# The layer norm's mean matmuls and factors moved behind the third backward tile in a two-way scan

## The chip, the cores and the metric

The kernel runs on one core of a Trainium2 chip. Its engines are TensorE (PE, with weight loads shown apart as PEld), VectorE (DVE), ScalarE (ACT), GpSimd (POOL) and SyncE (SP, which here only issues transfers); each works through its own instructions in order and waits for the others by semaphores. The metric is the device time of one execution in microseconds, as the median of three runs. Lower is better.

## The reference, cut to what matters

The program computes four residual blocks on x of shape (32, 192, 56, 56) in float32: an agent attention, an RWKV scan, a sparse shift with a 3x3 filter, and a long convolution. Each has a group norm ahead of it. The edit lies in the second block, the scan. With the tokens of an image in rows, N = 56*56 = 3136 of them and 192 channels:

```python
k, v, r = xs @ Wk.T, xs @ Wv.T, xs @ Wr.T          # xs: group-normed x
x_fwd = wkv_scan(real_w, u, k, v)                  # along the tokens
x_bwd = flip(wkv_scan(real_w, u, flip(k), flip(v)))
h = sigmoid(r) * 0.5 * (x_fwd + x_bwd)
mu, var = mean(h, -1), var(h, -1)                  # over the 192 channels
h = (h - mu) * rsqrt(var + 1e-5) * ln_g + ln_b
x = x + h @ Wo.T
```

The scan is a linear recurrence along the tokens: each output is a ratio of two running sums with decay exp(w), one of exp(k)*v and one of exp(k).

## The kernel before, in words

The stage is `scan_pairs` (from L898). Channels lie on the 128 partitions and tokens along the free axis. Images are taken in 16 pairs. One pair's 2 x 192 channels make three tiles of 128 partitions: tile 0 and tile 1 are the first 128 channels of the two images, tile 2 holds the last 64 channels of both. Tokens are cut into four chunks of 784 (MC), a chunk into two halves of 392 for PSUM's banks. A matrix product over channels comes in two parts: `outer` (L875) makes tiles 0 and 1, with lines L881 and L884, and `inner` (L886) makes tile 2, with L891 and L894.

Three generators or functions do the work of one chunk:

- `forwards` (L1135) loads x and normalises it on ACT (L1100), multiplies by Wk and Wv, takes exp(k) on ACT (L1149, tile `ek`) and exp(k)*v on DVE (L1154, tile `bv`), scans both (L1118, L1120 on DVE, with one-column copies on POOL at L1113 and L1119), inverts the denominator by a logarithm and an exponential on ACT (L1125, L1126) and multiplies (L1164).
- `backwards` (L1166) does the same from the right with the stored `ek` and `bv`, and takes the gate r: product with Wr, then three ACT operations (L1178, L1182, L1183) for the sigmoid. DVE then forms h in three operations per tile (L1186, L1187, L1188). It yields twice: after tiles 0 and 1, and after tile 2, "the third backward tile".
- `finish` (L1191) does the layer norm and the output product for the chunk that went through `backwards` a step earlier. It loads x, multiplies h by a centring matrix, squares on ACT (L1203, tile `sq`), multiplies the squares by a matrix of 1/192 (`mean_w`), makes the factors 1/sqrt(var) on ACT by a logarithm and an exponential (L1212, L1213, tile `rd`), and copies two 64-partition parts for tile 2 by transfers issued from ACT's queue (L1216). After a yield it multiplies h by the output matrix (`wog`), scales by the factors (L1226, DVE), adds bias and x with a running sum (L1229, DVE) and stores from SP's queue (L1243). It hands back functions that square the result on ACT (L1236) for the next block's group norm.

The main loop (from L1266) runs 16 pairs times four chunks, 64 steps; each step combines `backwards` of a chunk, `finish` of the chunk before and `forwards` of the next pair's chunk, in this order:

```python
next(back)
if ending is not None:
    next(ending)
next(back)
left = next(ending) if ending is not None else []
if ahead is not None:
    forwards(ahead, i, left)
```

In two of the four steps of a pair the group statistics of the pair before are gathered as well (L1079 to L1081, L1045 to L1048, L1026 to L1040), and once `conclude` stores them (L1250 to L1257).

This order is the one in which the operations are written. A scheduler orders each engine's instructions from it, by its own estimates, so neighbouring parts of one step are mixed on each engine. Tiles come from rotating pools: x from 7 buffers, `g`, `sq` and `rd` together from 9, PSUM from four buffers of two banks (`turned`). A load of x waits in SP's queue until the last reader of its buffer is done, and what stands behind it in that queue waits too.

Of the kernel before, what the change touches and what calls it, by code (L numbers as in the profile page):

```python
# [897 lines left out]
def scan_pairs(ctx: ExitStack, tc: tile.TileContext, a, k, x1, st_a, st_c, x2, rs2, wogT, count):  # L898
# [18 lines left out]
    def turned():  # L917
        ps = pp.tile([128, 2, BANK], F32, name="ps", tag="ps")
        return ps, ps[:, :, :HM], [ps[:, h, :HM] for h in range(2)]

    def parts(t):
        return [t[:, h * HM : (h + 1) * HM] for h in range(2)]
# [67 lines left out]
    def of(t):  # L990
        return slice(0, 1) if t < 2 else slice(1, 2)
# [13 lines left out]
    def load(p, m):  # L1005
        xs = [wp.tile([128, MC], F32, name="x", tag="x", bufs=7) for _ in range(3)]
        for r, t, ap in views(p, m):
            nc.sync.dma_start(out=xs[t][r], in_=ap)
        return xs
# [181 lines left out]
    def finish(s, m):  # L1191

        h, xs = s.y[m], load(s.p, m)
        hs = [parts(t) for t in h]
        sq = [wp.tile([128, MC], F32, name="sq", tag="t") for _ in range(3)]
        for tiles in ((0, 1), (2,)):
            ps = [turned() for _ in tiles]
            if len(tiles) == 2:
                pairs.outer(centre, [q[2] for q in ps], hs)
            else:  # L1200
                pairs.inner(centre, ps[0][2], hs)
            for t, (_, both, _) in zip(tiles, ps):
                nc.scalar.activation(  # L1203
                    sq[t].rearrange("p (h n) -> p h n", h=2), both, AF.Square,
                    accum_out=s.seen[:, 4, 3 * m + t : 3 * m + t + 1],
                )
        sqs = [parts(t) for t in sq]
        pv = [turned() for _ in range(2)]
        pairs.outer(mean_w, [q[2] for q in pv], sqs)
        rds = [wp.tile([128, MC], F32, name="rd", tag="t") for _ in range(3)]  # L1210
        for t, (_, both, _) in enumerate(pv):
            nc.scalar.activation(rds[t].rearrange("p (h n) -> p h n", h=2), both, AF.Ln, bias=eps)  # L1212
            nc.scalar.activation(rds[t], rds[t], AF.Exp, scale=-0.5)  # L1213

        for t, r in enumerate((slice(0, 64), slice(64, 128))):
            nc.scalar.dma_start(out=rds[2][r], in_=rds[t][r])  # L1216
        yield
        left = []
        for tiles in ((0, 1), (2,)):
            po = [turned() for _ in tiles]  # L1220
            if len(tiles) == 2:
                pairs.outer(wog, [q[2] for q in po], hs)
            else:
                pairs.inner(wog, po[0][2], hs)
            for t, (_, out, _) in zip(tiles, po):
                nc.vector.tensor_tensor(  # L1226
                    sq[t].rearrange("p (h n) -> p h n", h=2), out, rds[t].rearrange("p (h n) -> p h n", h=2), ALU.mult
                )
                nc.vector.scalar_tensor_tensor(  # L1229
                    xs[t], sq[t], cb[:, of(t)], xs[t], ALU.add, ALU.add, accum_out=s.sums[:, t, m : m + 1]  # L1230
                )
                if m == NM - 1:
                    nc.vector.tensor_scalar(s.away[:, t], s.sums[:, t, m : m + 1], -1.0 / MC, None, ALU.mult)

                def square(t=t):
                    nc.scalar.activation(  # L1236
                        sq[t], xs[t], AF.Square, bias=s.away[:, t], accum_out=s.squares[:, t, m : m + 1]
                    )

                left.append(square)  # L1240
        rows = slice(m * MC // S, (m + 1) * MC // S)
        for r, t, i, c in places:
            nc.sync.dma_start(out=x2[c, i, rows, s.p], in_=xs[t][r].rearrange("p (h w) -> p h w", w=S))  # L1243
        yield left
# [21 lines left out]
    for p in range(NP):  # L1266
        ahead = State(p + 1) if p + 1 < NP else None
        for i in range(NM):
            m = NM - 1 - i
            back, ending = backwards(s, m), None  # L1270
            if i > 0:
                ending = finish(s, m + 1)
            elif before is not None:
                ending = finish(before, 0)
# [7 lines that stand above are left out]
            else:  # L1282
                for later in left:
                    later()
            if before is not None:
                if i == 1:
                    before.spread = deviations(*moments_of(before), sp, "2")
                elif i == 2:
                    conclude(before)
        before, s = s, ahead  # L1290
    ending = finish(before, 0)
    next(ending)
    for later in next(ending):
# [587 lines left out]
```

## Time and profile before

| what | value |
|---|---|
| median of three runs | 12442.48 us (12437.2 to 12442.61) |
| the profiled execution's own time | 12448.77 us |
| its span, first to last instruction | 12447.0 us |
| granted TensorE clock, mean over the span | 0.96 |
| scan stage, start and end in the span | about 5052 to 8510 us |
| its regular part, 56 of the 64 steps | 5362 to 8350 us |
| transfers in that part | 99 GB/s, 0.40 of the DMA engines' time |

Times in the profile are microseconds from the span's start. An engine's row in the timeline gives start, length, engine, line, operation and the tiles it writes and reads; a bracket gives the idle time of the engine just ahead of the row and what ended it. Names stand without buffer numbers, so `ps` is any PSUM tile. Neighbouring instructions of an engine overlap by about 0.1 us, which is why a step from start to start is a little shorter than a length. The 56 steps form 14 rounds of four, and every round has the same order of instructions on DVE.

### The profile page before, as it was taken

How to read it: one execution, taken by the hardware profiler on the slowest of the kernel's cores; microseconds unless marked ns; L12 is line 12 of the kernel's file. 1: busy time of each engine (PE TensorE's matmuls, PEld its weight loads, DVE VectorE, ACT ScalarE, POOL GpSimd, SP SyncE). 2: the span in 40 equal slices, each digit the busy share in tenths (PEclk: the TensorE clock that was granted, in tenths of full speed). 3: DMA queues.
4: the chain of work that ended last, by engine and by line, in shares of the span. 5: the costliest groups of instructions: out<-in, count | busy, mean ns of one | idle time of the engine just before them, and what ended most of it. 6: DMA issues, size and time to landing. Idle time of an engine off the chain costs nothing. (4 is left out here: it accounts for less than half of the span.)

```text
span 12447.0 us, 164748 instructions
## 1 busy us (share of the span) xinstructions
PE 11356.6 (91%) x62738; PEld 7114.0 (57%) x62738; DVE 10861.2 (87%) x15560; ACT 6217.0 (50%) x11820; POOL 2303.7 (19%) x2237
## 2 busy tenths in 40 slices
PE   4999999999999999788888888888999999999999
PEld 1555555555555655333333333335777777777777
DVE  3888888888888888799999999997888888888888
ACT  2555555555555555466666666663333333333333
POOL 0000000000000000465555565552000000000000
PEclk7999999999999999899999999998999999999999
DMA  2111111111111111233444343432111111111111
GB/s 65 32 50 40 40 40 40 40 40 42 54 43 40 40 40 32 73 98 96 102 102 100 95 98 97 102 98 77 42 44 42 42 44 42 45 42 43 42 43 29
DMA packets 940870, 719.51 MB, mean 58 GB/s; under 512 B 777295, under 2 KB 818746, under 8 KB 931057
## 3 DMA queue, kind: packets, MB, share of 16 engines
q1 hardware_dynamic: 929832, 683.18, 21.3%
q10 hardware_dynamic: 10240, 25.70, 0.8%
q8 instruction: 500, 8.19, 0.3%
q14 instruction: 298, 2.43, 0.1%
HBM read 403.11 MB, written 240.80 MB: 52 GB/s over the span
## 5 line engine op out<-in xcount | busy, mean ns | idle before, releaser
L591 DVE SCALAR_TENSOR_TENSOR o<-v_a,dww,o 128x896 f32<-128x896 f32 (+1 forms) x1024 | 1056.9, 1032 | 408.1 <-ACT v_a L565 291.8
L1807 ACT COPY y<-ps 64x252 f32<-64x252 f32 (+1 forms) x2376 | 809.6, 341 | 1134.3 <-PE ps L1801 1104.0
L1725 PE MATMUL ps<-f,real 84*84 84x112 f32 x6144 | 1090.8, 259 | 0.0
L1725 PE MATMUL ps<-f,imag 84*84 84x112 f32 x6144 | 1089.4, 259 | 0.0
L1732 ACT COPY z<-ps 84x448 f32<-84x448 f32 x768 | 406.2, 529 | 1217.1 <-PE ps L1725 1215.6
L859 POOL MEMSET Wk_cc<- 128x128 f32 x1 | 0.2, 205 | 4819.7 <-DVE x_c L757 4819.7
L1725 PEld LDWEIGHTS ps<-f,real 84*84 84x84 f32 x6144 | 783.9, 153 | 134.2 <-issue 95.8
L1725 PEld LDWEIGHTS ps<-f,imag 84*84 84x84 f32 x6144 | 763.8, 153 | 0.0
L1125 ACT ACTIVATE q<-q 128x784 f32<-128x784 f32 x384 | 328.7, 856 | 808.9 <-DVE q L1120 637.8
L881 PE MATMUL ps<-sq,mean_aa 128*128 128x392 f32 x512 | 301.7, 753 | 424.6 <-ACT sq L1203 424.6
L591 DVE SCALAR_TENSOR_TENSOR o<-v_c,dww,o 128x448 f32<-128x448 f32 (+1 forms) x1024 | 638.5, 623 | 5.2
L604 PE MATMUL ps<-xs_a,gk_a 128*98 128x448 f32 (+1 forms) x1536 | 639.6, 497 | 0.0
L605 PE MATMUL ps<-xs_c,gk_c 125*98 125x448 f32 (+1 forms) x1536 | 633.1, 493 | 0.0
L608 ACT ACTIVATE pr<-ps,low 98x896 f32<-98x896 f32 (+1 forms) x384 | 352.3, 918 | 557.1 <-DVE low L606 557.1
L1591 POOL TENSOR_TENSOR mat<-tap,tap 114x114 f32<-114x114 f32 x96 | 40.8, 425 | 3166.6 <-PE ps L1651 2313.1
L696 PE MATMUL ps<-gq_a,xs_a 128*112 128x294 f32 x1792 | 603.3, 418 | 19.0 <-DVE pq L701 19.0
L1742 PE MATMUL ps<-z,f 84*114 84x448 f32 x1536 | 608.9, 539 | 0.0
L697 PE MATMUL ps<-gq_c,xs_c 125*112 125x294 f32 x1792 | 595.1, 413 | 0.0
L1699 PE MATMUL re<-y,f 128*84 128x420 f32 (+1 forms) x1152 | 532.2, 542 | 8.8 <-ACT y L1807 7.7
L1801 PEld LDWEIGHTS ps<-f,padded 114*128 114x128 f32 x3168 | 473.3, 192 | 96.7 <-issue 70.3
L1699 PE MATMUL im<-y,f 128*84 128x420 f32 (+1 forms) x1152 | 526.9, 538 | 0.0
L1801 PE MATMUL ps<-f,padded 114*128 114x168 f32 x3168 | 503.7, 310 | 21.6 <-DVE o L1744 10.2
(397 smaller groups left out, 29260.2 us busy)
## 6 DMA issues: line engine op xcount, KB each, us to landing
x<-x SPq DMA_DIRECT2D x512, 392.0 KB
x<-x SPq DMA_DIRECT2D x512, 196.0 KB
x<-x SPq DMA_DIRECT2D x192, 399.0 KB
out_x<-x SPq DMA_DIRECT2D x384, 196.0 KB
x_a<-in_x SPq DMA_DIRECT2D x32, 1568.0 KB
x<-x_a SPq DMA_DIRECT2D x32, 1568.0 KB
x_c<-in_x SPq DMA_DIRECT2D x64, 392.0 KB
x<-x_c SPq DMA_DIRECT2D x64, 392.0 KB
```

The lines of the kernel that those rows point to most:

```text
L591: nc.vector.scalar_tensor_tensor(dst, tap(i), dww[:, t, i : i + 1], dst, ALU.mult, ALU.add)
L604: mm(ps[P2, h, :n], g[:, cols], xs_a[j][:, px], start=True, stop=False)
L605: mm(ps[P2, h, :n], gk_c[0:KC, 2 * j + h, cols], xs_c[j][0:KC, px], start=False, stop=True)
L608: nc.scalar.activation(pr[:, :, :n], ps[P2, :, :n], AF.Exp, bias=low[:, j, p : p + 1], accum_out=sums[:, j, p : p + 1])
L696: mm(ps[:SUB, i, :HA], xs_a[j][:, px], g, start=True, stop=False)
L697: mm(ps[:SUB, i, :HA], xs_c[j][0:KC, px], gq_c[0:KC, 2 * j + (q + i) // ns], start=False, stop=True)
L1699: nc.tensor.matmul(ps[:, : n * 84], f2[:, i, :], y[:, i0 : i0 + n].rearrange("p g s u -> p (g s u)"), start=True, stop=True)
L1725: nc.tensor.matmul(ps[:84, i * 2 * S : (i + 1) * 2 * S], part[:, i0 + i].rearrange("p s u -> p (s u)"), f3[:, m, :], start=(m == 0), stop= ...
L1732: nc.scalar.copy(z[:, i0 : i0 + n].rearrange("p g m w -> p (g m w)"), ps[:84, : n * 2 * S])
L1742: nc.tensor.matmul(got, f4[:, m, :], z[:, i0 : i0 + n, m, :], start=(m == 0), stop=(m == 1))
L1801: nc.tensor.matmul(ps[:, g * 168 : (g + 1) * 168], flat[:, (g0 + g) * 128 : (g0 + g + 1) * 128], f1, start=True, stop=True)
L1807: nc.scalar.copy(y[64 * m : 64 * m + 64, 2 * g0 + i : 2 * (g0 + n) : 2], got[64 * i : 64 * i + 64, :, :, m, :])
```

## The change

One `yield` in `finish` moves up: from behind the factors and their copies to ahead of the mean's matmuls. So the first part of `finish`, written ahead of the third backward tile, now ends with the centring and the squares, and the mean's matmuls, the two logarithms and two exponentials and the two copies are written after that tile, just ahead of the output product.

```diff
                     sq[t].rearrange("p (h n) -> p h n", h=2), both, AF.Square,
                     accum_out=s.seen[:, 4, 3 * m + t : 3 * m + t + 1],
                 )
+        yield
         sqs = [parts(t) for t in sq]
         pv = [turned() for _ in range(2)]
         pairs.outer(mean_w, [q[2] for q in pv], sqs)
...
         for t, r in enumerate((slice(0, 64), slice(64, 128))):
             nc.scalar.dma_start(out=rds[2][r], in_=rds[t][r])
-        yield
         left = []
         for tiles in ((0, 1), (2,)):
```

In the changed kernel the lines of the moved part are one higher (L1213, L1214, L1217); from the output product on the numbers are as before. The scheduler works on the new order, so the order of neighbouring instructions on ACT, DVE and POOL changes as well.

## The prediction

> **What bounds the kernel now.** First the page, for the engines' shares; then the busy time by stage, to find the stage that the edit touches; then VectorE's (DVE's) waits inside it; last the timeline of one step, engine by engine.
>
> The page, first lines (busy us, share, instructions):
>
> ```profile
> span 12447.0 us, 164748 instructions
> ## 1 busy us (share of the span) xinstructions
> PE 11356.6 (91%) x62738; PEld 7114.0 (57%) x62738; DVE 10861.2 (87%) x15560; ACT 6217.0 (50%) x11820; POOL 2303.7 (19%) x2237
> ```
>
> PE leads over the whole, but the edit lies in the scan stage only. Busy time of its regular middle (start:end, length, then busy us by engine):
>
> ```profile
> 5362.00:8350.00 2988.00, 2485.15 (x9132) 1135.18 (x9130) 2903.91 (x2998) 1908.15 (x3278) 1725.80 (x1496) 0.93 0.40 99
> ```
>
> Here DVE is busy 2903.91 of 2988 us: the stage lasts as long as DVE's work, which the edit leaves alone, plus DVE's idle time, some 84 us. So the edit is worth what it does to DVE's waits there. These are (total, times, longest):
>
> ```profile
> DVE sq L1226 <- PE ps L884: 51.5, 39, 2.1
> DVE p L1186 <- ACT q L1126: 12.7, 22, 1.0
> DVE q L1118 <- ACT ek L1149: 10.2, 16, 0.7
> ```
>
> The stretch holds 14 rounds of four steps (A, B, C, D by how the third backward tile, tile 2, and the group statistics fall); rounds last 213.4 us on average (2988/14). A, B and D each wait once, 1.4 to 1.9 us, for the output product (wog, L884) or just after it; C hardly waits; B waits 0.7 more at L1118. One D step shows why. Its DVE, ACT and PE rows (start, length):
>
> ```profile
> 6822.72 0.94 DVE L1188 TENSOR_TENSOR y<-y,g 128x784 f32<-128x784 f32 x1
> 6823.59 1.02 DVE L1120 SCALAR_TENSOR_TENSOR q<-ek,eu,q 128x784 f32<-128x784 f32 x1
> 6826.30 0.97 DVE L1226 TENSOR_TENSOR sq<-ps,rd 128x784 f32<-128x784 f32 x1 [1.68 <-ACT g L1182]
> 6827.19 0.97 DVE L1186 TENSOR_TENSOR p<-p,q 128x784 f32<-128x784 f32 x1
> ...
> 6833.64 1.03 DVE L1229 SCALAR_TENSOR_TENSOR x<-sq,cb,x 128x784 f32<-128x784 f32 x1
> 6834.60 0.08 DVE L1229 DVE_READ_ACCUMULATOR x<-sq,cb,x 128x1 f32 x1
> 6834.63 3.60 DVE L1118 TENSOR_TENSOR_SCAN q<-decay,f,ek 128x784 f32<-128x784 f32 x2
> ```
> ```profile
> 6811.88 5.47 PE L881 MATMUL ps<-sq,mean_aa 128*128 128x392 f32 x8 [6.63 <-ACT sq L1203]
> 6817.28 1.59 PE L884 MATMUL ps<-sq,mean_ca 64*128 64x392 f32 x8
> 6818.80 1.58 PE L891 MATMUL ps<-x,Wr_cc 128*128 128x392 f32 x4
> 6820.31 1.54 PE L894 MATMUL ps<-x,Wr_ac 128*64 128x392 f32 x8
> 6821.78 2.90 PE L881 MATMUL ps<-y,wog_aa 128*128 128x392 f32 x8
> 6824.61 1.59 PE L884 MATMUL ps<-y,wog_ca 64*128 64x392 f32 x8
> ```
> ```profile
> 6824.65 0.86 ACT L1125 ACTIVATE q<-q 128x784 f32<-128x784 f32 x1 [1.08 <-DVE q L1120]
> 6825.41 0.84 ACT L1182 ACTIVATE g<-g 128x784 f32<-128x784 f32 x1
> 6826.16 0.84 ACT L1126 ACTIVATE q<-q 128x784 f32<-128x784 f32 x1
> ...
> 6832.75 0.95 ACT L1236 ACTIVATE sq<-x,away 128x784 f32<-128x784 f32 x1 [1.18 <-DVE x L1229]
> ```
>
> PE idles 6.63 us for the squares (L1203), then runs mean, Wr of tile 2 and wog in a row; wog ends at 6826.20, and DVE's L1226 starts at 6826.30 (the releaser named, L1182, ended just as late; the other steps name PE). But tile 2's reciprocal is hardly earlier: L1125, L1126, then DVE's L1186.
>
> **The change part by part.** No instruction is added or dropped; the built programs give the orders, here of a D step, with the tile in brackets (L1213, L1214, L1217 of the changed kernel are L1212, L1213, L1216 of the rows):
>
> ```
> DVE now  L1188(1) L1120(2) L1226(0) L1186(2) L1229(0) L1187(2) L1226(1) L1188(2) L1229(1) L1226(2) L1229(2) L1118
> DVE new  L1120(2) L1188(1) L1186(2) L1226(0) L1187(2) L1229(0) L1188(2) L1226(1) L1226(2) L1229(1) L1229(2) L1118
> ACT now  L1125(1) L1126(1) L1212 x2 L1213 x2 copies L1178(2) L1125(2) L1182(2) L1126(2) L1183(2) L1100 x2 L1236(0) L1100 L1236(1) L1149 x2 L1236(2)
> ACT new  L1125(1) L1178(2) L1126(1) L1182(2) L1100 L1183(2) L1213 x2 L1214(0) L1125(2) L1214(1) L1126(2) copies L1100 x2 L1236(0,1,2) L1149 x2
> ```
>  Steps are start to start, from the rows: DVE L1186, L1187, L1188, L1226 0.89 each, L1120 and L1229 0.95, scan 1.76; ACT 0.75 each, L1203 and L1178 0.80, L1100 0.94, L1236 0.95. Three latencies: L1125 starts 0.04 after L1120's end; L1186 0.97 after L1126 starts (6612.67 to 6613.64, where L1186 waited); L1118 0.93 after L1149 starts (6728.51 to 6729.44).
>
> *PE.* Tile 2's Wr goes ahead of the mean, into the 6.63 us gap. 1.58 + 1.54 us leave the stretch from squares to wog; L1226 would find wog 3 us sooner, so its wait on PE, up to 2.1 us, goes. Late next is ACT.
>
> A clock point, not needed below: the first eight mean matmuls take 5.47 us after the 6.63 us gap, the eight of wog 2.90. [...]
>
> *ACT, tile 2's reciprocal.* In A, B and D the new order is: L1178, L1126, L1182, L1100, L1183, (L1100), L1213 twice, then L1125 and L1126 of tile 2 with a factor's Exp (L1214) between; the factors stand ahead of it and end before DVE asks. From the end of tile 2's L1120, L1186 can start 0.04 + 0.76 + 0.75 + 0.97 = 2.52 later, as now, where L1182 stands between. DVE's new order puts L1186 ahead of L1226, and L1188 of tile 1 behind L1120 as sole cover, where L1226 used to stand. For D: L1120 at 6822.71 (L1188 of tile 1 now comes behind it), end 6823.73, L1188 ends its turn at 6824.52, L1186 starts at 6826.25: idle 1.73, against 1.68 now. A: 1.49 (L1257 covers 0.24), B 1.57 (L1048). C has L1253 and one L1226 as cover: 0.6, against 0 now. So **the wait on PE turns into a wait on ACT**.
>
> *ACT, the end of the step.* New on DVE: in A, B and D both last L1226 come ahead of both last L1229, so x of tiles 1 and 2 is finished late and close together. ACT squares them (L1236) ahead of the next state's exponential (L1149), in A and D all three squares first (now two). D on: L1186 6826.25, L1226 6827.14, L1187 6828.03, L1229 6828.91, L1188 6829.86, L1226 6830.75 and 6831.64, L1229 6832.53 and 6833.48. L1236 of tile 1 starts 1.07 after its L1229 (as 6831.68 to 6832.75): 6833.60; tile 2 6834.55; L1149 6835.50; L1118 6836.43. Now: 6834.63. **D loses 1.80 us**. The same working for the others:
> - A (L1120 at 6662.14): L1186 6665.69, last L1229 6672.91. Moments (L1080) now stand ahead of the scans and wait for the last L1236 (6673.98 to 6675.02): the five small operations end 0.87 later, both scans and L1120 take 5.37, L1154 at 6681.3 against 6680.55: +0.77.
> - B (6716.22): L1186 6719.77, last L1233 done 6728.15, L1236, L1149 6729.13, L1118 6730.06 against 6729.44: +0.62.
> - C: only the 0.6 at L1186: +0.60.
>
> A round: 3.79. These rows are of a round of 213.53, 0.12 over the mean, so 3.91; times 14, 54.7 us. The irregular steps: one before the 14 rounds is like D, +2; in the last backward step the 9.08 us wait of L1226 on PE shrinks by the 3 us of Wr: -3. **Sum +54 us.**
>
> *What stays hidden, with its bounds.* (1) L1100 of two forward tiles comes up ahead of the factors; its loads sit in SP's queue until tile 2's Wr has read the buffers (SP issues at 6714.25, Wr_cc ran 6712.59 to 6714.1). Wr moves up, so they are issued some 10 us sooner and land about 3.5 us later (issue 6775.09, L1100 in ACT 6778.56): cost 0. If they came no sooner than now, ACT would stand some 6 us past need, 1.5 of it slack: 4.5 x 56 = 250 us. I take 0, since the release moves. (2) The rd copies (ACT's queue, L1217) are issued after ACT passes tile 2's reciprocal, some 4.6 us ahead of the last L1226 in A and B; no row gives their landing apart. By the loads' 3.5 us they cost nothing; 1 us past need would cost 28 in A and B together. I take 0. (3) PSUM: wog of tile 1 takes Wr's bank, freed by L1178 before 6818: nothing.
>
> Against the runs: the profiled execution took 12448.77 (span 12447.0), 6.3 above the median 12442.48. So 12502.8 by its own time, 12496 on the scale of the runs.
>
> **Rivals.**
> 1. *Nothing takes the wait's place* (faster). DVE loses its waits at L1226, L1186 and L1118: 56.9 + 12.0 + 10.8 in the stretch, 3 at the end: 12360. It decides if L1186 of tile 2 can start within some 1 us of L1120's end. For: the PE wait is real and largest. Against: three ACT turns, 2.52 us, already show L1186 waiting 22 times.
> 2. *Only the exchange at L1186, the end of the step unharmed* (L1149 not behind the squares in time): A -0.27, B -1.16, C +0.60, D -0.01, so with the 0.12: -0.72 x 14 and -1: 12431, no change by measure. Against: ACT works in order, and A and D place three squares ahead.
> 3. *Loads late in ACT's queue*: +250 us, 12690. Against: (1) above.
> 4. *It does not do what it says*: the scheduler keeps the old order; 12442. Against: the built order has moved.
>
> **How the numbers follow.** Forecast 0.70, rivals 0.08, 0.15, 0.04, 0.03. Its own range is 12470 to 12530 (up: the copies late). The range leaves out rivals 1 and 3 (0.12) and reaches to rival 2: 12425 to 12530. 0.2%, 25 us, is about what a measurement can tell here: faster 0.09, same 0.17, slower 0.74.
>
> **What would show it.** Right: no wait of L1226 on PE; L1186 waits on L1126 in every A, B, D, about 1.5 us; L1118 waits on L1149 in B and D, L1080 on L1236 in A, 1 us; rounds of 217.3. Wrong: L1100 waiting on DMA, L1226 on the rd copy, or rounds of 208 to 213.

## The result, and the profile after

The changed kernel takes 12486.51 us (median of 6 runs, 12484.01 to 12499.9) against 12442.98 us (6 runs, 12437.2 to 12452.77): a ratio of 1.0037, 95% interval 1.0024 to 1.005, so it is slower by 30 to 62 us. It was run again later beside new runs of the kernel before (first experiment): 1.0039 (1.0025 to 1.0053).

The page of the changed kernel has nearly the engine times of before; DVE is 4.5 us less busy in a span 38 us longer:

```profile
span 12485.2 us, 164581 instructions
...
PE 11385.3 (91%) x62738; PEld 7095.6 (57%) x62738; DVE 10856.7 (87%) x15560; ACT 6203.9 (50%) x11820; POOL 2236.6 (18%) x2237
```

The same 56 regular steps, as one stretch (start:end, length, busy us of PE, PEld, DVE, ACT and POOL, then the granted clock, the DMA share and GB/s):

```profile
5352.00:8392.00 3040.00, 2525.22 (x9134) 1124.56 (x9134) 2900.35 (x2997) 1899.01 (x3277) 1664.45 (x1496) 0.96 0.40 97
```

DVE is busy about as long as before, 2900 us for 2904, and the stretch is 52 us longer: all of that is idle time of DVE, 140 us in place of 84. DVE's waits there (total, times, longest), first in the kernel before, over the 56 steps alone (the prediction's list began 62 us earlier, so two of its totals are a little larger), then in the changed kernel:

```profile
DVE sq L1226 <- PE ps L884: 50.8, 38, 2.1
DVE p L1186 <- ACT q L1126: 11.8, 21, 1.0
DVE q L1118 <- ACT ek L1149: 10.2, 16, 0.7
DVE sq L1226 <- ACT g L1182: 3.4, 2, 1.7
DVE sq L1226 <- ACT q L1125: 2.7, 3, 0.9
```
```profile
DVE p L1186 <- ACT q L1126: 72.3, 56, 1.6
DVE q L1118 <- ACT ek L1149: 51.8, 28, 1.9
DVE mv L1080 <- ACT sq L1236: 12.7, 14, 0.9
```

The wait of L1226 on PE is gone, and there are only waits on ACT. By place, L1226 and L1186 together waited 68.7 us before and L1186 waits 72.3 now, so that exchange is about even; the waits at the end of the step (L1118, L1080) grew from 10.2 to 64.5. A D step shows both places, DVE first (start, length, last bracket the wait):

```profile
6838.00 1.03 DVE L1120 SCALAR_TENSOR_TENSOR q<-ek,eu,q 128x784 f32<-128x784 f32 x1
6838.95 0.96 DVE L1188 TENSOR_TENSOR y<-y,g 128x784 f32<-128x784 f32 x1
6841.54 0.98 DVE L1186 TENSOR_TENSOR p<-p,q 128x784 f32<-128x784 f32 x1 [1.63 <-ACT q L1126]
6842.43 0.97 DVE L1226 TENSOR_TENSOR sq<-ps,rd 128x784 f32<-128x784 f32 x1
...
6848.76 1.03 DVE L1229 SCALAR_TENSOR_TENSOR x<-sq,cb,x 128x784 f32<-128x784 f32 x1
...
6851.70 3.59 DVE L1118 TENSOR_TENSOR_SCAN q<-decay,f,ek 128x784 f32<-128x784 f32 x2 [1.91 <-ACT ek L1149]
```

ACT and PE of the same step:

```profile
6839.06 0.86 ACT L1125 ACTIVATE q<-q 128x784 f32<-128x784 f32 x1 [1.65 <-DVE q L1120]
6839.83 0.84 ACT L1214 ACTIVATE rd<-rd 128x784 f32<-128x784 f32 x1
6840.57 0.84 ACT L1126 ACTIVATE q<-q 128x784 f32<-128x784 f32 x1
...
6849.83 0.95 ACT L1236 ACTIVATE sq<-x,away 128x784 f32<-128x784 f32 x1
...
6850.78 0.80 ACT L1149 ACTIVATE ek<-ps 128x784 f32<-128x784 f32 x1
```
```profile
6827.18 4.59 PE L881 MATMUL ps<-sq,mean_aa 128*128 128x392 f32 x8 [3.50 <-ACT sq L1203]
...
6836.05 1.59 PE L884 MATMUL ps<-y,wog_ca 64*128 64x392 f32 x8
```

PE has wog ready at 6837.64, almost 5 us before L1226 uses it at 6842.43; that gain shows in the rows. But DVE stands at L1186 for tile 2's reciprocal: three ACT operations behind L1120, with one DVE operation (L1188) to cover them. At the end of the step the last L1229 starts at 6848.76; ACT squares its result from 6849.83, turns to L1149 only at 6850.78, and DVE scans from 6851.70.

Steps start to start, means over the 14 rounds (regular part: 56 steps):

| | A | B | C | D | round | shortest and longest round | regular part |
|---|---|---|---|---|---|---|---|
| before | 54.06 | 54.18 | 51.99 | 53.18 | 213.41 | 212.90, 214.58 | 2987.7 |
| after | 54.82 | 55.01 | 52.40 | 54.90 | 217.13 | 217.11, 217.15 | 3039.8 |
| difference | 0.76 | 0.83 | 0.41 | 1.72 | 3.72 | | 52.1 |

The last but one column is a further sign that PE is off the path: before, rounds differed by up to 1.7 us, in part with the mean's matmuls ahead of wog (an A step took about 53.96 us when the first eight of them took 4.6 us, and 54.1 to 54.4 when they took 5.6); after, the rounds all agree within 0.04, though those matmuls vary at least as much (last section).

### The profile page after: what moved, and what is told of

Read it like the earlier page. It is cut to its first block, busy times and chain, and to the rows that moved or that the text cites. A ratio compares the mean times of both kernels' runs of the same rounds, so it can differ in the third digit from the quotient of the medians.

```text
span 12485.2 us, 164581 instructions
## 1 busy us (share of the span) xinstructions
PE 11385.3 (91%) x62738; PEld 7095.6 (57%) x62738; DVE 10856.7 (87%) x15560; ACT 6203.9 (50%) x11820; POOL 2236.6 (18%) x2237
## 5 line engine op out<-in xcount | busy, mean ns | idle before, releaser
L1125 ACT ACTIVATE q<-q 128x784 f32<-128x784 f32 x384 | 328.5, 855 | 813.1 <-DVE q L1120 615.8
L709 ACT ACTIVATE pq<-pq 112x1176 f32<-112x1176 f32 x224 | 265.3, 1184 | 503.5 <-DVE pq L701 380.5
```

## The experiments

The theory to be tested (T1 below): the price of the change is two places in ACT's order. In one, DVE's L1186 follows tile 2's L1120 too closely; in the other, the squares L1236 stand ahead of the exponentials L1149 that the scans need. The rivals (R1 to R5) stand in the expectations. "Ratio" is to the kernel before run beside it, with its 95% interval.

| kernel | time, us | ratio | a round | regular part |
|---|---|---|---|---|
| changed kernel again | 12495.7 | 1.0039 (1.0025 to 1.0053) | 217.13 | 3039.9 |
| `ek_first` | 12435.1 | 0.9993 (0.9984 to 1.0002) | 212.98 | 2981.7 |
| `before_ek_first` | 12424.2 | 0.9987 (0.9978 to 0.9996) | 212.28 | 2972.0 |
| `squares_ahead` | 12496.3 | 1.0045 (1.0031 to 1.0059) | 217.49 | 3044.9 |
| `recip_adjacent` | 12599.3 | 1.0119 (1.0104 to 1.0135) | 223.59 | 3130.3 |
| `gate_first` | 12371.5 | 0.9938 (0.9925 to 0.9952) | 208.97 | 2925.6 |
| `gate_first_ek_first` | 12337.2 | 0.9915 (0.9902 to 0.9929) | 206.50 | 2891.0 |

The ACT edits use one device: a dependence for the scheduler alone, without a semaphore, that says which of two ACT instructions comes first (`behind_of(what, ahead)`).

**The changed kernel again.** No edit.

> The changed kernel once more, beside the kernel before. T1 (what the change costs is two waits that ACT's order makes in the scan stage, at L1186 and at the end of the step): +52 us in the scan stage again, a total of +43 to +55; the 10 us by which the attention stage ahead of it was shorter in the first profile is a difference between executions and need not return. R3 (the move also makes the attention stage 10 us shorter, by placement or code): that stage is 10 us shorter again, and the total +43.

Measured: 12495.73 us, 51.5 over the 12444.19 of the kernel before beside it. The regular part is 3039.9 us, as in the first profile. The attention stage, which comes ahead of the scan stage, ends at 5008 us in the span, as in the kernel before (5007), not at 4997 as in the first profile of the changed kernel. So the scan stage costs 51 us, and the 10 us of the attention stage were a difference between executions; R3 falls.

**The end of the step, undone in the changed kernel (`ek_first`).**

```diff
-                        nc.scalar.activation(
+                        made = nc.scalar.activation(
...
-                        later()
+                        later(made)
...
-                def square(t=t):
-                    nc.scalar.activation(
+                def square(ahead=None, t=t):
+                    done = nc.scalar.activation(
...
+                    if ahead is not None:
+                        behind_of(done, ahead)
```

The first activation is L1149, `later` is the function that squares (L1236).

> The changed kernel, but on ACT all three squares of the next block's norm (L1236) stand behind both exponentials of the next state (L1149). T1: the end-of-step waits go (L1118 on L1149 1.91 in D and 1.79 in B, L1080 on L1236 0.91 in A), the waits of L1186 stay at 1.5 to 1.6; a round of 217.1 becomes 212.5, the whole 64 us less: about 12422. R1 (what ends last there is PE: the product with Wk stands behind a PSUM buffer that L1226 gives back late, so L1149 is late whatever ACT does): the wait of L1118 stays at 1 us or more, now put down to PE, and the time stays above 12460. Since scans start sooner, something else may wait later in the step; by T1 nothing does.

Measured: 12435.1 us. DVE's waits in the regular part (L1191 and L1131 are L1186 and L1126 of the changed kernel), and C's row:

```profile
DVE p L1191 <- ACT q L1131: 84.6, 56, 1.6
```
```profile
6761.05 0.98 DVE L1191 TENSOR_TENSOR p<-p,q 128x784 f32<-128x784 f32 x1 [1.39 <-ACT q L1131]
```

Every wait at the end of the step is gone, R1 with them, and those of A, B and D at L1186 stay to the hundredth (1.49, 1.55, 1.63). The time is 13 us above the forecast for a reason that the forecast had missed: in C the scheduler now puts L1226 behind L1186, so that one operation of cover is lost, and the wait is 1.39 for 0.51; 14 x 0.88 = 12.3 us.

**The same edit in the kernel before (`before_ek_first`).** The diff is that of `ek_first`, on the kernel before.

> The kernel before with the same edit on ACT as in ek_first: both exponentials L1149 ahead of the squares L1236; DVE's order is that of the kernel before. T1: only B's 0.71 at L1118 goes, the waits of L1226 on PE (1.4 to 1.9 in A, B, D) stay; a round of 213.4 becomes 212.7, the time 10 us less: 12434. Then ek_first (12435), the same with the mean moved, stands level with it: with the squares out of the way the move gives up PE's wait and takes ACT's for nothing, and the whole price of the change is the end of the step. R5 (freeing PE of its wait was worth something by itself, hidden by the squares): this kernel is slower than ek_first by 20 us or more, 12455 or above.

Measured: 12424.16 us, 16 us less than before, and 11 us less than `ek_first` (7 us by the two ratios, each to its own kernel before). R5 falls; T1 had the two kernels level, and missed by these 7 to 11 us. DVE's waits in the regular part (L1231, L1191 and L1131 are L1226, L1186 and L1126 of the kernel before):

```profile
DVE sq L1231 <- PE ps L884: 53.3, 42, 2.1
DVE p L1191 <- ACT q L1131: 12.6, 21, 1.0
```

B's wait at L1118 is gone, PE's waits have stayed. Without the squares in the way, the move of the mean costs 2981.7 - 2972.0 = 9.7 us: it changes 66 us of listed waits (PE's at L1226 and some of ACT's) for 85 of ACT's, while DVE's busy time falls by 6 (2901.2 to 2895.0). By steps, A, B and D are each 0.2 shorter, and C is 1.36 longer, 19 us over the 14 rounds, for the cover that it lost. So in A, B and D the exchange at L1186 is about even, and the end of the step is the larger part of the price: 52.1 - 9.7 = 42 of the 52 us by these pairs, each kernel from one profile. That is a low figure. Of C's 19 us, 12 come from the reordering in `ek_first` (a wait of 1.39 for 0.51), which the change itself does not cause. Without them the exchange costs nothing and the end of the step is all of the price, as the waits by place already say (68.7 to 72.3, and 10.2 to 64.5).

**The end of the step alone, in the kernel before (`squares_ahead`).** L1149 of tile 0 stands behind the last square; the mean and the factors stay where they were.

```diff
+                if wt is wk and tiles == (0, 1):
+                    squared = [later() for later in behind]
...
+                        if t == 0 and squared:
+                            behind_of(made, squared[-1])
```

> The kernel before with one part of the change's effect alone: the mean and the factors stay where they were, but on ACT all three squares L1236 stand ahead of L1149. T1: L1118 starts 1.07 + 0.95 + 0.93 = 2.95 after the start of the last L1229, which is 2.0 after its end: about 2.0 of new wait in C and in D, about 1.3 more in B, and 0.9 at L1080 in A; the waits of L1226 on PE stay at 1.4 to 1.9. A round 6 us longer, the time 12443 + 87 = 12530 (12490 to 12560, as the scheduler moves other operations a little). R1 (L1149 is late for another reason, the squares only stand beside it): no wait at L1118 above 0.7, time within 12 us of 12443.

Measured: 12496.3 us, so 51 us slower, not 87. That is inside the stated range, but not for the stated reason. The waits (L1123, L1156, L1235, L1242, L1192, L1131 are L1118, L1149, L1229, L1236, L1186, L1126 of the kernel before), then a D step's end, DVE and ACT rows in order of time:

```profile
DVE q L1123 <- ACT ek L1156: 80.2, 42, 1.9
DVE p L1192 <- ACT q L1131: 43.9, 29, 1.6
DVE mv L1080 <- ACT sq L1242: 12.7, 14, 0.9
```
```profile
6850.01 1.03 DVE L1235 SCALAR_TENSOR_TENSOR x<-sq,cb,x 128x784 f32<-128x784 f32 x1
...
6852.96 3.59 DVE L1123 TENSOR_TENSOR_SCAN q<-decay,f,ek 128x784 f32<-128x784 f32 x2 [1.91 <-ACT ek L1156]
```
```profile
6851.08 0.95 ACT L1242 ACTIVATE sq<-x,away 128x784 f32<-128x784 f32 x1 [1.99 <-DVE x L1235]
...
6852.03 0.80 ACT L1156 ACTIVATE ek<-ps 128x784 f32<-128x784 f32 x1
```

The chain is there to the hundredth: 1.07 from L1229 to the square, 0.95 to L1149, 0.93 to the scan, 2.95 in all, in the kernel before as in the changed one; the wait is 1.91 at L1118 in B, C and D, and 0.91 at L1080 in A. So R1 of this run falls. What failed is the other half of the expectation: PE's waits did not stay, since the scheduler put other operations on DVE and ACT in another order as well (in A and B L1186 waits in place of L1226). So this run shows the size of the chain, and not a clean total.

**Nothing between the reciprocal's two ACT operations (`recip_adjacent`).**

```diff
+            done = nc.scalar.activation(rds[t], rds[t], AF.Exp, scale=-0.5)
+            if by is not None:
+                behind_of(done, by.last)
```

`by.last` is tile 2's L1126. The same two lines stand behind the normalisation of x (L1100).

> The changed kernel, but on ACT nothing stands between the logarithm and the exponential of tile 2's reciprocal (L1125, L1126 of the changed kernel): the second factor's exponential and two of the normalisations of x come behind it. T1: L1186 can start 0.04 + 0.89 + 0.97 = 1.90 after L1120's end in place of 2.52, so its wait falls by 0.6 in A, B and D (1.49, 1.55, 1.63 to 0.87, 0.93, 1.01); in C the scheduler puts L1226 behind L1186, so that one cover is lost: 0.51 + 0.89 - 0.62 = 0.78. In C it also puts all three squares ahead of L1149, so T1 has a new wait of about 1.8 at L1118 there. A round: 217.1 - 1.86 + 0.27 + 1.8 = 217.3, the same time as the changed kernel, 12490. R1 (PE or a transfer ends the wait at L1186 or at the L1226 behind it): L1186 waits as long as before, or L1226 takes what it gains; no new wait in C.

Measured: 12599.3 us, 109 us over the forecast. L1186 (here L1195) waits longer, not shorter. In these rows L1125, L1127, L1133, L1158, L1197 and L1105 are L1118, L1120, L1126, L1149, L1188 and L1100 of the changed kernel:

```profile
DVE q L1125 <- ACT ek L1158: 108.4, 49, 3.0
DVE p L1195 <- ACT q L1133: 104.7, 56, 1.9
```
```profile
6905.86 0.94 DVE L1197 TENSOR_TENSOR y<-y,g 128x784 f32<-128x784 f32 x1
6906.73 1.03 DVE L1127 SCALAR_TENSOR_TENSOR q<-ek,eu,q 128x784 f32<-128x784 f32 x1
6909.66 0.98 DVE L1195 TENSOR_TENSOR p<-p,q 128x784 f32<-128x784 f32 x1 [1.90 <-ACT q L1133]
```
```profile
6912.76 4.30 PE L881 MATMUL ps<-x,Wk_aa 128*128 128x392 f32 x8 [5.67 <-ACT x L1105]
```

The chain is as short as T1 said, 1.90 from the end of L1120 to L1186, and ACT still ends the wait, so R1 of this run falls. But the scheduler, with the other order on ACT, put L1188 ahead of L1120: the only cover is gone, and DVE waits the chain's whole length. The expectation had overlooked this. DVE also waits longer at L1118 (7.7 us a round, against 3.7 in the changed kernel). Part of that is x: held back on ACT, it leaves PE idle for 5.67 us ahead of Wk, and in every second A and C ACT then waits about 1 us for PE's L884 ahead of L1149. In B, where DVE waits 2.7 to 3.0 us, ACT goes almost straight from the squares to L1149, so there it is the squares again. Two steps of the expectation failed, the order on DVE and what comes late at the end of the step; the chain's length is the part that stands.

**The mean moved half as far (`gate_first`).** On the kernel before: Wr and the sigmoid of tile 2 come ahead of the mean, tile 2's scan behind the factors. The first added `yield` is in `backwards`, behind the sigmoid and ahead of tile 2's scan; the second is in `finish`, behind the squares (the one behind the copies stays); the rest is in the main loop.

```diff
+                if t == 2:
+                    yield
...
+        yield
...
             next(back)
             if ending is not None:
                 next(ending)
             next(back)
+            if ending is not None:
+                next(ending)
+            next(back)
```

> The kernel before with the mean and the factors moved by half as far: tile 2's product with Wr and its sigmoid come ahead of the mean, but the factors stay ahead of tile 2's scan, so that on DVE two L1226 and two L1229 lie between tile 2's L1120 and its L1186 (cover 3.7 us and more against the 2.52 of ACT's chain). T1: no L1226 waits for PE, no L1186 waits; what is left is L1118 behind the squares, 1.0 in D, 1.9 in B, 0.2 in A; a round of 210.6, 40 us less than before: about 12403. R2 (it is the earlier product with Wr, or the loads that follow it, that costs): the time is above the kernel before's 12443, as in the changed kernel. Rival 1 of the prediction (nothing waits any more): 12360.

Measured: 12371.5 us, 73 us faster than before (ratio 0.9938). DVE's only wait in the regular part, and a D step, DVE and then ACT (L1229, L1232, L1188, L1190, L1239 are L1226, L1229, L1186, L1188, L1236 of the kernel before):

```profile
DVE q L1118 <- ACT ek L1149: 28.6, 28, 1.0
```
```profile
6785.21 1.02 DVE L1120 SCALAR_TENSOR_TENSOR q<-ek,eu,q 128x784 f32<-128x784 f32 x1
6786.15 0.96 DVE L1190 TENSOR_TENSOR y<-y,g 128x784 f32<-128x784 f32 x1
6787.04 1.83 DVE L1229 TENSOR_TENSOR sq<-ps,rd 128x784 f32<-128x784 f32 x2
6788.80 1.01 DVE L1232 SCALAR_TENSOR_TENSOR x<-sq,cb,x 128x784 f32<-128x784 f32 x1
...
6790.71 0.96 DVE L1188 TENSOR_TENSOR p<-p,q 128x784 f32<-128x784 f32 x1
...
6796.30 3.60 DVE L1118 TENSOR_TENSOR_SCAN q<-decay,f,ek 128x784 f32<-128x784 f32 x2 [1.02 <-ACT ek L1149]
```
```profile
6794.43 0.95 ACT L1239 ACTIVATE sq<-x,away 128x784 f32<-128x784 f32 x1 [2.57 <-DVE x L1232]
...
6795.37 0.80 ACT L1149 ACTIVATE ek<-ps 128x784 f32<-128x784 f32 x1
```

Wr is moved as in the changed kernel and PE's wait is gone as there; the difference is that five DVE operations (4.5 us) now lie between L1120 and L1186, and L1186 does not wait. So neither the earlier Wr nor its loads show a cost in any wait of DVE, and R2 falls. The forecast of 12403 was 32 us too high: it had given D a wait of 1.0, B 1.9 and A 0.2 at the end of the step. B places only two squares ahead of L1149, and both are done early; the waits are those of C and D, 1.02 each (the chain's 1.91 less one L1188 of cover, 0.89). That makes 15 of the 32 us; with it go a DVE busy time 11 us lower than before (2892.9 for 2903.9) and some 10 us outside the regular part, which were not traced further.

**Both edits (`gate_first_ek_first`).** The diffs of `gate_first` and `ek_first` together.

> Both edits that worked: the mean and the factors between tile 2's product with Wr and tile 2's scan, and on ACT the squares L1236 behind both exponentials L1149. T1: the two waits left in the first of them (L1118 on L1149, 1.02 in C and in D) go, and no L1186 waits, since the order of DVE there stays; a round of 208.98 becomes 206.9, the regular part 29 us shorter: about 12343. R4 (with DVE never waiting, PE becomes the bound, or the squares, now late, hold back buffers that the next step's loads need): new waits of 0.5 us or more a step, time 12371 or more.

Measured: 12337.2 us, 6 us below the forecast, 108 us faster than the kernel before (ratio 0.9915) and 149 us than the first runs of the changed one. In the regular part no wait of DVE is listed at all:

```profile
5349.00:8240.00 2891.00, 2492.28 (x9130) 1116.70 (x9128) 2888.59 (x2997) 1884.44 (x3277) 1731.50 (x1496) 0.96 0.43 102
```

DVE is busy 2888.6 of 2891.0 us: the stage is now as long as DVE's work. R4 falls. With both of ACT's waits taken away, nothing is left of the price, and moving Wr ahead of the mean is worth more than the prediction's first rival gave it (12360), if the two places on ACT are seen to. Of the surplus of 23 us, 15 are DVE's busy time, 2888.6 against 2903.9 before: nearly every kind of operation is a little shorter (L1120 takes 1018 ns on average for 1024, its scans 1827 to 1839 for 1834 to 1846). Why is not shown.

## Why the prediction was right

The prediction gave 12496 us; measured were 12486.5 and, the second time, 12495.7. Its steps:

- *DVE bounds the stage, its idle time is what changes.* Right: DVE's busy time is the same in both, and the stretch has grown by DVE's idle time.
- *PE's wait at L1226 goes.* Right: no such wait is listed in the regular part.
- *L1186 waits for L1126 in its place.* Right, with the three latencies: 1.49, 1.55 and 1.63 in A, B and D (1.49, 1.57 and 1.73 forecast). That the exchange costs little was in the working too, as the second rival's sum shows (-0.72 a round). `gate_first`, with more cover, and `recip_adjacent`, with none, move this wait as the chain says: 0, and 1.90 in B, C and D.
- *The end of the step.* Right: 1.91 in D and 1.79 in B at L1118, 0.91 in A at L1080; `ek_first` removes all of them by the order on ACT. The closing list of signs says 1 us for these waits, which is short for B and D; the prediction's own working, with the last L1229 done at 6834.51 and L1118 at 6836.43, gives 1.92 in D.
- *The sums.* A 0.76 (0.77 forecast), D 1.72 (1.80). B 0.83 against 0.62 and C 0.41 against 0.60 are mis-sized by 0.2 with opposite signs; both were worked out from one sampled round, in which B was 0.2 longer than its mean (54.40 against 54.18), so B's error is that of the sample. In C L1186 waits 0.51 for the 0.6 forecast, and 0.1 of idle time that was there before is gone. A round 3.72 (3.91 forecast with the correction for the sampled round), the regular part 52.1 us (54.7).
- *The irregular steps.* The D-like one +1.8 (2 forecast). Another early step, which the prediction did not count, is 1.7 shorter: L1154 waits 1.69 for PE in place of 3.35. The end was put at -3, but the last steps, behind the 56, are only 1.1 us shorter: L1226's long wait shrank from 9.08 to 5.03, and a new wait of 2.58 stands at L1188. These three make -1.0 with a forecast of -1, so that part of the sum came out right by luck.
- *The clock point, outside the sum.* In the D steps shown PE's gap shrank from 6.63 us to 3.50, and the first eight matmuls of the mean took 4.59 us for 5.47, at a mean granted clock of 0.63 for 0.52; the eight of wog took 2.90 in both, at 1.00. No wait of DVE on PE was left for these 0.9 us to shorten.
- *What was costed at nothing.* The loads, the copies and PSUM: no wait of DVE on a transfer is listed, ACT's L1100 waits 0.5 us at most, and the three waits listed make 137 of DVE's 140 us of idle time. The copies' landing was not measured by itself.
- *The rivals.* "Nothing takes the wait's place" and "only the exchange" did not happen. The second is near what `ek_first` and `before_ek_first` show when the squares are put behind: the exchange alone costs 10 us between them; the cover lost in C is 19, and A, B and D win 9 back. The first, no wait left at all, is what `gate_first_ek_first` shows, with another order.

The first runs' median is 10 us below the forecast: the attention stage was shorter by that in the profiled execution and not in the second one, which no term of the sum was meant to catch. The scan stage alone came out 51 to 52 us longer, for the 54 forecast.

## What to carry to other kernels

An earlier operand is worth only what the next latest one allows: before moving work to free one wait, follow every operand of the waiting engine's next instructions, with the operations that stand between on the engine that makes them. Where a scheduler orders the engines, moving one part regroups its neighbours on all of them, and the price may lie at the other end of the step. A hand-over from DVE to ACT and back can be hidden by placing other work of DVE between (4.5 us of it in `gate_first`, where L1186 no longer waits), or by putting what the waiting engine needs ahead of what nobody waits for; the second was one small edit and repaired the step's end in both kernels.

## What the runs showed of the hardware that was not expected

The first eight matmuls of the mean, after PE's gap for the squares, last 2.90 us or up to 5.60, and the gap's length alone does not tell which. Rows of the changed kernel and then one of `gate_first` (the bracket is the gap):

```profile
5579.16 5.60 PE L881 MATMUL ps<-sq,mean_aa 128*128 128x392 f32 x8 [3.41 <-ACT sq L1203]
6013.43 2.90 PE L881 MATMUL ps<-sq,mean_aa 128*128 128x392 f32 x8 [3.41 <-ACT sq L1203]
```
```profile
6043.08 4.59 PE L881 MATMUL ps<-sq,mean_aa 128*128 128x392 f32 x8 [1.87 <-ACT sq L1205]
```

With the same gap of 3.41 us they took 2.90 and 5.60, and 4.59 after a gap of 1.87. In the changed kernel's two rows the granted clock differs as the times do. Here is the stretch of each (start:end, length, busy us of PE, PEld, DVE, ACT and POOL, then the granted clock, the DMA share and GB/s):

```profile
5579.16:5584.76 5.60, 5.60 (x10) 2.60 (x10) 5.60 (x7) 4.19 (x10) 5.38 (x4) 0.50 0.14 57
6013.43:6016.33 2.90, 2.90 (x10) 1.51 (x10) 2.90 (x5) 1.56 (x4) 2.73 (x3) 1.00 0.28 108
```

The eight slow ones ran at 0.50, the eight fast ones at 1.00. The D steps shown lie between: 4.59 us at 0.63 in the changed kernel (from 6827.18), 5.47 at 0.52 in the kernel before (from 6811.88). What made the clock differ after equal gaps was not shown. It did not matter to this change, since PE's work was no longer last.

A hand-over between DVE and ACT, where the one engine waited for the other, took nearly the same time in the kernels named: L1126 to L1186 0.96 to 0.98 us from start to start (before, changed, `recip_adjacent`), L1149 to the scan 0.92 or 0.93 (before, changed, `squares_ahead`, `gate_first`), the last L1229 to its square 1.06 to 1.09 (before, `squares_ahead`, `gate_first`). The whole turn from the end of L1120 to L1186 through two ACT operations took 1.90 us with nothing between them (`recip_adjacent`) and 2.51 with a factor's exponential (changed kernel, D), so by these numbers it needs two to three of DVE's own operations of 0.89 as cover.
